# Two VectorE transposes moved behind a projection's additions in a paged-attention kernel

## The chip, the cores and the metric

The kernel runs on one core of a Trainium2 chip. The time is device microseconds (us) of one execution of the whole program; the median of three runs is taken. A separate execution is profiled, and times within it are counted from the start of its span.

## The reference

Two layers are added to x (8 sequences of 128 tokens, width 512, float32). The first is a projection by an adapter chosen for each sequence, followed by a small mixture of low-rank experts. The second, which takes nearly all of the time, is attention over a paged cache, followed by a gated low-rank network. The attention, cut to what matters:

```
q = x Wq  (32 heads of 128)    k = x Wk,  v = x Wv  (8 heads of 128)
q, k = rope(rmsnorm(q)), rope(rmsnorm(k))
k_all = concat(k_cache[block_table], k)        # 512 cached + 128 new keys
scores = q k_all / sqrt(128), cached keys beyond cache_seqlens masked
o = softmax(scores) v_all                      # v_all likewise
attention = o Wo                               # 32*128 -> 512
```

Four query heads share one key and value head.

## The kernel before

The attention is cut into 64 units (NU = 64): a unit is one sequence and one key head with its four query heads. `iteration(u)` (from line 1418 on) issues everything of unit u, and pieces of its neighbours, in an order written out by hand. Nothing reorders it later: each engine takes its instructions in the order of the program, and each waits at its own semaphores. TensorE is PE below, VectorE is DVE, ScalarE is ACT, GpSimd is POOL and SyncE is SP.

A unit has a loop `for h in range(REP)` over its four heads ("slots" 0 to 3). In a slot,

- `scores(u, h)` (lines 439 and 442) has PE multiply one head's queries with 512 cached and 128 new keys, into one of two PSUM tiles that take turns;
- `mask_exp(u, h)` (line 452) has DVE scale, mask and find the lowest value, and ACT take the exponential and its sum (line 463);
- `normalize(u, h - 1)` has DVE take the reciprocal of the previous head's sum (line 468) and POOL multiply by it (line 469);
- `blocks(u, h - 2)` (line 474) has DVE transpose a finished head's probabilities in blocks of 32, into the tile pb;
- `output(u - 3, h)` (line 1148) has PE multiply an older unit's result with a quarter of Wo;
- `project(k, j, slots[h - 1 : h])` has PE compute one of seven products of later units' q, k and v (line 262, two matmuls with half of the contraction each, recorded as four), and DVE add it from PSUM into the sums that it belongs to (line 265). Seven products stand for eight, as in Strassen's scheme. In slots 1, 2 and 3 these are the products 1, 2 and 6 in the odd units, and 4, 5 and 3 in the even ones; product 7 comes at the end of the odd units. Product 2 needs one addition, product 5 needs two.

In slot 2, `new_pb(u)` takes the tile pb. There is one such tile, so its first writer waits until the previous unit's transfer out of it is done. `blocks_qk(u + 2, u)` (line 425) is that first writer: DVE transposes the rotated queries and the key of unit u + 2 in blocks into it. `blocks(u, 0)` follows.

After the loop come the last reciprocal, the last two heads' blocks, `exchange_out(u)` and the rotation of unit u + 3 (lines 329 to 347). `exchange_out` writes pb to a tile px in DRAM, half from SP's and half from ACT's queue (line 486). In the next iteration `exchange_in` reads it back by SP's queue, reordered: qkb (line 1000), from which ACT makes the transposed queries of unit u + 2 (line 1010), and pT (line 1003), the transposed probabilities, which PE multiplies with the values two units later (line 1023). SP also loads the cached keys of the next sequence's units, kt, page by page (line 193): five or so ahead of `exchange_in` and three behind it in the odd units. POOL gathers the values (line 203), computes the sums of the weights' quarters (line 163) and of x, and issues the loads of weights.

Of the kernel before, what the change touches and what calls it, by code (L numbers as in the profile page):

```python
# [58 lines left out]
def adaln_ffn_kernel(  # L59
# [115 lines left out]
    def load_o(hf, *parts):  # L175

        for i, to in parts:
            nc.gpsimd.dma_start(out=wo_t[:, to], in_=wo[hf, i])
# [35 lines left out]
    def bank(tag, name):  # L214
        return ps_1.tile([P, DM], F32, tag=tag, name=name)
# [11 lines left out]
    NU = len(units)  # L227
# [25 lines left out]
    def project(k, j, products):  # L253

        pr, g = k % (B // 2), k // (B // 2) * GH + j
        key = k, j
        for i in products:
            x, y, tag = PRODUCTS[i]
            ps = bank(tag, f"p_{k}_{j}_{i}")[:, :HW]
            w = wq_t[g][:, y].rearrange("p (c n) -> p c n", c=2)  # L260
            for c in range(2):
                nc.tensor.matmul(  # L262
                    out=ps, lhsT=xo[:, pr, x, c, :], rhs=w[:, c, :], start=(c == 0), stop=(c == 1)
                )
            add = lambda out, a: nc.vector.tensor_tensor(out, a, ps, ALU.add)  # L265
            if i == 1:
                part_t[key] = pj.tile([P, HW], F32, tag="u", name=f"u_{k}_{j}")
                nc.scalar.copy(part_t[key], ps)
                c_t[4 * k + j] = pj.tile([P, 2 * HW], F32, tag="c0", name=f"c0_{k}_{j}", bufs=2)
                c_t[4 * k + 2 + j] = pj.tile([P, 2 * HW], F32, tag="c1", name=f"c1_{k}_{j}", bufs=2)  # L270
            u, c0, c1 = part_t[key], c_t[4 * k + j], c_t[4 * k + 2 + j]
            if i == 2:
                add(c0[:, :HW], u)
            elif i == 6:
                add(u, u)
            elif i == 7:
                add(c1[:, HW:], u)
            elif i == 4:
                add(c1[:, :HW], c1[:, HW:])
            elif i == 5:  # L280
                add(c1[:, HW:], c1[:, HW:])
                add(c0[:, HW:], u)
            elif i == 3:
                add(c0[:, HW:], c0[:, HW:])
# [71 lines left out]
    def transpose_qk(u, home=None):  # L356

        qk = qk_t.pop(u)
        t = banks(f"tq_{u}", 1 if u < 2 else None)
        for h in range(NH):  # L360
            nc.tensor.transpose(
                t[:, h * S : (h + 1) * S], qk[:, h].rearrange("p t d -> p (t d)"), ident
            )
        if home is None:
            home = pj.tile([P, NH * S], F32, tag="qkT", name=f"qkT_{u}", bufs=2)
        nc.scalar.copy(home, t[:, : NH * S])
        qkT_t[u] = home.rearrange("p (h s) -> p h s", h=NH)
# [55 lines left out]
    def blocks_qk(u, w):  # L423

        nc.vector.transpose(  # L425
            pb_t[w][:, :, PW:].rearrange("p i (h a) -> p h i a", a=32),
            qk_t.pop(u).rearrange("p h t d -> p h (t d)").rearrange(
                "p h (i a) -> p h i a", a=32
            ),
        )  # L430
# [3 lines left out]
    def scores(u, h, which=None):  # L434
        st, g = units[u]
        kt, _ = kv_t[st]
        qkT = qkT_t[u]
        s = banks(f"s_{u}_{h}", which)
        nc.tensor.matmul(  # L439
            out=s[:, :L], lhsT=qkT[:, h, :], rhs=kt[:, :, g % GH, :], start=True, stop=True  # L440
        )
        nc.tensor.matmul(  # L442
            out=s[:, L:NK], lhsT=qkT[:, h, :], rhs=qkT[:, REP, :], start=True, stop=True
        )
        s_t[u, h] = s

    def mask_exp(u, h):

        st, g = units[u]
        p = pp.tile([P, NK], F32, tag="p", name=f"p_{u}_{h}")  # L450
        low = stat.tile([P, 1], F32, tag="low", name=f"low_{u}_{h}")
        nc.vector.tensor_tensor_reduce(  # L452
            out=p,
            in0=s_t.pop((u, h))[:, :NK],
            in1=mask_t[st],
            scale=rs_t[u][:, h : h + 1],
            scalar=BIG,
            op0=ALU.add,
            op1=ALU.min,
            accum_out=low,  # L460
        )
        den = stat.tile([P, 1], F32, tag="den", name=f"den_{u}_{h}")
        nc.scalar.activation(p, p, AF.Exp, bias=low, scale=-1.0, accum_out=den)  # L463
        p_t[u, h], den_t[u, h] = p, den

    def normalize(u, h):
        den = den_t.pop((u, h))
        nc.vector.reciprocal(den, den)  # L468
        nc.gpsimd.tensor_scalar(p_t[u, h], p_t[u, h], den, 1.0, ALU.mult, ALU.mult)  # L469

    def blocks(u, h):

        w = (LC + 1) * 32
        nc.vector.transpose(  # L474
            pb_t[u][:, :, h * w : (h + 1) * w].rearrange("p i (j a) -> p j i a", a=32),
            p_t.pop((u, h)).rearrange("p (j i a) -> p j i a", i=QD, a=32),
        )
# [370 lines left out]
    def f_fold():  # L848

        nc.vector.tensor_copy(fw_t["s"], fw_t["f"])  # L850
# [141 lines left out]
    with ExitStack() as l1:  # L992
# [352 lines left out]
        def f_turn_of(b):  # L1345
            yT_t[b] = f_turn(b, *room(b))
# [71 lines left out]
        def iteration(u):  # L1418
            nonlocal room2

            on = lambda v: 0 <= v < NU
# [65 lines left out]
            for h in range(REP):  # L1487
                if on(u):
                    if (u, h) not in ((1, 0), (1, 1), (2, 0)):
                        scores(u, h)  # L1490
                        mask_exp(u, h)
                    if h > 0 and (u, h) != (1, 1):
                        normalize(u, h - 1)

                    if (u, h) == (1, 2):
                        transpose_qk(3)

                    sums_o(u, h)
                    sums_w(u, h)
                    if 16 <= u < NU - 8 and (r, h) == (2, 3):  # L1500
                        load_o(u // 16, (1, B12))

                    if h == 2:
                        new_pb(u)
                        if u + 2 in range(4, NU):
                            blocks_qk(u + 2, u)
                    if h > 1:
                        blocks(u, h - 2)
                    if h == 1 and u == NU - 5:
                        f_fold()  # L1510
                    if u == NU - 5 and h == 1:
                        t4 = wo_t[:, 6, : 2 * (E1 + HN)].rearrange("p (c n) -> p c n", c=2)
                        fw_t["qa"], qa_steps[:] = quarters_of(
                            fw_t["a"],
                            *quarter_rooms(wo_t[:, 5]),
                            t4[:, :, E1:],
                            t1_room.rearrange("p (c n) -> p c n", c=2),
                        )
                        sa = fw_t["sa"]
                        fw_t["qa"][M1], fw_t["qa"][M2] = (sa[:, c : c + 2, : E1 + HN] for c in (0, 2))  # L1520
                        fw_t["qa"][M4] = t4
                    at = (u - NU + 5, h)
                    if at == (1, 0):
                        nc.vector.tensor_copy(fw_t["qa"][M4][:, :, :E1], fw_t["s"][:, 2:])
                    if at in ((0, 1), (0, 2), (1, 0), (1, 1)):
                        qa_steps.pop(0)()
                    if u in GATED and h == 1:
                        f_add(GATED[u])
                    if u in GATED and h == 2:
                        f_mult(GATED[u])  # L1530
                    if h == 3:
                        z_blocks(u)
                    if h == 2 and u in FIRST:
                        f_turn_of(2 * FIRST[u])
                    if u in REST:
                        if h == 1:
                            f_turn_of(2 * REST[u] + 1)
                        elif h > 1:
                            f_step(REST[u], 2 * h - 4, 2 * h - 3)
                elif u in GATED and u < NU + 2:  # L1540
                    if h == 1:
                        f_add(GATED[u])
                    elif h == 2:
                        f_mult(GATED[u])
                    elif h == 3:
                        z_blocks(u)
                if on(u - 3):
                    output(u - 3, h)
                    sums_a(u - 3, h)
                if u in REST and h == 3:  # L1550
                    f_rest_products(REST[u], 0)
                if h > 0 and slots:
                    project(k, j, slots[h - 1 : h])

                if (u, h) in WHOLE:
                    project_whole(1, *WHOLE[u, h])
# [220 lines left out]
```

## Time and profile before

| what | value |
| --- | --- |
| runs | 1198.29, 1198.89 and 1201.55 us; median 1198.89 |
| the profiled execution | 1203.57 us, of which its span is 1201.8 us |
| granted clock of PE | 1.0 throughout |
| PE busy from 174 to 1054 us | 874.36 of 880 us |
| DVE busy in the same stretch | 720.22 us |
| POOL busy in the same stretch | 613.75 us |
| DMA share in the same stretch | 0.85 |
| DVE transposes of line 425, from 174 to 1054 us | 54, median 826 ns |
| DVE transposes of line 474, from 174 to 1054 us | 216, median 826 ns |
| DVE additions of line 265, from 174 to 1054 us | 189 of 128x384, medians 518 to 553 ns |

The stretch from 174 to 1054 us is given because units 5 to 58 lie in it; unit 4 has its first scores at 160.0 us. In rows of the order of time, the first column is the start and the second the duration; a bracket at the end holds the engine's idle time ahead of the row and what ended it. In lists of waits the three numbers are the sum, the number of times and the longest, the first and the last in us. The ends of matmuls are modelled, and their starts are not.

### The profile page before, as it was taken

The page shows a single profiled execution, that of the slowest core. Times are in us where ns is not written, and L with a number is a line of the kernel's source. Part 1 is how long each engine was busy: PE and PEld are TensorE (multiplying, and loading weights), DVE is VectorE, ACT ScalarE, POOL GpSimd, SP SyncE. Part 2 cuts the span into 40 slices and gives each one's busy share as a digit, 9 for nine tenths or more (in the row PEclk, how much of TensorE's full clock was granted, in tenths as well). Part 3 has the DMA queues.
Part 4 walks back from the last instruction along what each step waited for, and adds up shares of the span by engine and source line. Part 5 has one row for each costly group of instructions (what it writes and reads, how often), then busy time and mean ns, then how long its engine had stood idle before and what let it go on. Part 6 is the DMA issues. An engine that isn't in the chain of part 4 may idle for free.

```text
span 1201.8 us, 17007 instructions
## 1 busy us (share of the span) xinstructions
PE 1188.7 (99%) x4196; PEld 721.8 (60%) x4196; DVE 936.6 (78%) x2141; ACT 509.3 (42%) x1469; POOL 771.6 (64%) x867
## 2 busy tenths in 40 slices
PE   9999999999999999999999999999999999999998
PEld 7766555565655556555555555565655555655567
DVE  2557788787978887878888787878888888897757
ACT  1345544444444444434444344444444444444321
POOL 3554879778746676678656685677656684765432
PEclk9999999999999999999999999999999999999999
DMA  8823787888779978898889978888789878888643
GB/s 316 312 72 119 249 248 241 265 281 281 235 248 262 322 239 272 269 287 273 248 254 286 276 241 282 284 272 267 245 256 303 274 249 252 270 289 262 197 153 114
DMA packets 205447, 302.35 MB, mean 252 GB/s; under 512 B 84771, under 2 KB 119332, under 8 KB 204324
## 3 DMA queue, kind: packets, MB, share of 16 engines
q1 hardware_dynamic: 170164, 196.29, 53.2%
q10 hardware_dynamic: 18864, 52.57, 13.4%
q0 software_dynamic: 16320, 52.40, 12.5%
q8 instruction: 34, 0.56, 0.2%
q14 instruction: 65, 0.53, 0.1%
HBM read 185.44 MB, written 115.74 MB: 251 GB/s over the span
## 4 chain that ended last, share of the span: by engine, by line
PE 82%; DMA 5%; DVE 4%; POOL 4%; issue 2%; SPq 2%; ACT 1%; ACTq 0%; DVEq 0%; POOLq 0%
PE o L1023 18%; PE p L262 17%; PE s L439 15%; PE y L1148 12%; PE s L442 4%; DMA kt<-in_kc 3%; PE p L295 3%; PE cp L627 2%; PE bp L649 2%; PE y L1161 2%; DMA px<-pb 2%; DVE pb L474 1%; POOL p L469 1%; SPq L192 1%; PE op L981 1%
## 5 line engine op out<-in xcount | busy, mean ns | idle before, releaser
L463 ACT ACTIVATE p<-p,low 128x640 f32<-128x640 f32 x256 | 211.9, 828 | 428.5 <-DVE den L468 268.9
L469 POOL TENSOR_SCALAR p<-p,den 128x640 f32<-128x640 f32 x256 | 210.2, 821 | 219.5 <-DVE den L468 218.3
L452 DVE CUSTOM_DVE_ANT_0 p<-s,mask,rs 128x640 f32<-128x640 f32 x256 | 222.8, 879 | 82.8 <-PE s L442 82.0
L262 PE MATMUL p<-wqkv,xo 128*128 128x384 f32 x784 | 281.0, 487 | 1.3 <-POOL wqkv L163 0.7
L439 PE MATMUL s<-kt,qkT 128*128 128x512 f32 x504 | 258.3, 594 | 4.7 <-DMA px<-pb 1.7
L1023 PE MATMUL o<-pT,vt 128*128 128x512 f32 x512 | 230.3, 592 | 0.0
L474 DVE STREAM_TRANSPOSE pb<-p 128x640 f32<-128x640 f32 x248 | 204.8, 826 | 24.8 <-POOL p L469 24.7
L1148 PE MATMUL y<-wo,oT 128*128 128x256 f32 x784 | 206.5, 380 | 1.2 <-DVE yp L1217 1.0
L262 PEld LDWEIGHTS p<-wqkv,xo 128*128 128x128 f32 x784 | 148.3, 190 | 70.7 <-POOL wqkv L163 1.9
L442 PEld LDWEIGHTS s<-qkT 128*128 128x128 f32 x504 | 95.8, 190 | 120.5 <-issue 120.5
L203 POOL DMA_INDIRECT vt<-in_vc,vrow x128 | 138.3, 1081 | 42.0 <-issue 30.1
L1023 PEld LDWEIGHTS o<-pT,vt 128*128 128x128 f32 x512 | 97.0, 190 | 108.0 <-issue 92.8
L439 PEld LDWEIGHTS s<-kt,qkT 128*128 128x128 f32 x504 | 94.5, 190 | 77.1 <-issue 33.9
L1148 PEld LDWEIGHTS y<-wo,oT 128*128 128x128 f32 x784 | 131.9, 191 | 10.1 <-PE s L442 1.5
L311 ACT ACTIVATE sq<-c 128x128 f32<-128x128 f32 x320 | 98.8, 309 | 9.5 <-DVE oT L474 1.4
L442 PE MATMUL s<-qkT 128*128 128x128 f32 x504 | 96.8, 274 | 0.0
L317 POOL TENSOR_TENSOR rs<-ss,mhalf 128x5 f32<-128x5 f32 x64 | 84.0, 1312 | 5.3
L1046 ACT COPY oT<-o 128x512 f32<-128x512 f32 x64 | 37.5, 585 | 111.0 <-PE o L1023 92.4
L315 POOL TENSOR_SCALAR ss<-ss,eps 128x5 f32<-128x5 f32 x64 | 23.4, 366 | 73.1 <-ACT sq L311 73.1
L265 DVE TENSOR_TENSOR c<-c,p 128x384 f32<-128x384 f32 x84 | 44.9, 534 | 26.7 <-PE p L262 26.7
L1023 PE MATMUL o<-pT,vn 128*128 128x512 f32 x128 | 65.4, 592 | 0.0
L425 DVE STREAM_TRANSPOSE pb<-ca 128x640 f32<-128x640 f32 x60 | 49.9, 832 | 14.5 <-DMA kt<-in_kc 8.9
(301 smaller groups left out, 1513.8 us busy)
## 6 DMA issues: line engine op xcount, KB each, us to landing
pT<-px SPq DMA_DIRECT2D x64, 1280.0 KB, 7.3
px<-pb SPq DMA_DIRECT2D x120, 400.0 KB, 5.5
px<-pb ACTq DMA_DIRECT2D x120, 400.0 KB, 5.5
qkb<-px SPq DMA_DIRECT2D x60, 320.0 KB, 3.6
kt<-in_kc SPq DMA_DIRECT2D x512, 32.0 KB, 4.8
wqkv<-in_wqkv POOLq DMA_DIRECT2D x32, 384.0 KB, 5.1
wo<-in_wo POOLq DMA_DIRECT2D x17, 512.0 KB, 7.7
yd<-yp POOLq DMA_DIRECT2D x12, 512.0 KB, 9.1
```

Of the source, the lines that this page charges most:

```text
L203: nc.gpsimd.indirect_dma_start(out=kv_t[step][1][:, c, :], out_offset=None, in_=vc, in_offset=bass.IndirectOffsetOnAxis(ap=vrow[:, hf, at ...
L262: nc.tensor.matmul(out=ps, lhsT=xo[:, pr, x, c, :], rhs=w[:, c, :], start=(c == 0), stop=(c == 1))
L311: nc.scalar.activation(sq, cs[:, at : at + D], AF.Square, accum_out=ss[:, h : h + 1])
L317: nc.gpsimd.tensor_tensor(rs, ss, mhalf, ALU.pow)
L439: nc.tensor.matmul(out=s[:, :L], lhsT=qkT[:, h, :], rhs=kt[:, :, g % GH, :], start=True, stop=True)
L442: nc.tensor.matmul(out=s[:, L:NK], lhsT=qkT[:, h, :], rhs=qkT[:, REP, :], start=True, stop=True)
L452: nc.vector.tensor_tensor_reduce(out=p, in0=s_t.pop((u, h))[:, :NK], in1=mask_t[st], scale=rs_t[u][:, h : h + 1], scalar=BIG, op0=ALU.add, ...
L463: nc.scalar.activation(p, p, AF.Exp, bias=low, scale=-1.0, accum_out=den)
L469: nc.gpsimd.tensor_scalar(p_t[u, h], p_t[u, h], den, 1.0, ALU.mult, ALU.mult)
L474: nc.vector.transpose(pb_t[u][:, :, h * w : (h + 1) * w].rearrange("p i (j a) -> p j i a", a=32), p_t.pop((u, h)).rearrange("p (j i a) -> ...
L1023: nc.tensor.matmul(out=o, lhsT=vt[:, c, j * D : (j + 1) * D] if c < LC else vn_t.pop(u), rhs=pT[:, c], start=(c == 0), stop=(c == LC),)
L1148: nc.tensor.matmul(out=y_t["y"][:, half * HN : (half + 1) * HN], lhsT=part(key)[:, i * S : (i + 1) * S], rhs=wo_t[:, slot(w, key[0] // (B ...
```

## The change

In the units 4 to 58 (`3 < u < NU - 5`) the two transposes of slot 2, `blocks_qk(u + 2, u)` and `blocks(u, 0)`, are issued after that slot's `output` and `project` in place of before them. On DVE, which takes part in `project` with its additions, this places the one or two additions of slot 2 ahead of the two transposes; the order of the other engines' instructions stays. The other units keep the old order.

```
                     if h == 2:
                         new_pb(u)
-                        if u + 2 in range(4, NU):
+                    behind = h == 2 and 3 < u < NU - 5
+                    if h > 1 and not behind:
+                        if h == 2 and u + 2 in range(4, NU):
                             blocks_qk(u + 2, u)
-                    if h > 1:
                         blocks(u, h - 2)
...
                 if h > 0 and slots:
                     project(k, j, slots[h - 1 : h])
 
+                if on(u) and behind:
+                    blocks_qk(u + 2, u)
+                    blocks(u, 0)
+
                 if (u, h) in WHOLE:
                     project_whole(1, *WHOLE[u, h])
```

## What was predicted, with its working

> **What bounds the kernel now.** I read the page's busy table first, then the list of what TensorE (PE) waited for in the stretch from 174 to 1054 us, which holds nearly all of the units 4 to 58 that the change touches, and then the order of time around one unit.
>
> ```profile
> PE 1188.7 (99%) x4196; PEld 721.8 (60%) x4196; DVE 936.6 (78%) x2141; ACT 509.3 (42%) x1469; POOL 771.6 (64%) x867
> ```
>
> ```profile
> PE s L439 <- DMA px<-pb: 1.7, 1, 1.7
> PE s L439 <- DMA kt<-in_kc: 1.6, 2, 1.2
> PE y L1148 <- DVE yp L1217: 1.0, 1, 1.0
> PE p L262 <- POOL wqkv L163: 0.7, 1, 0.7
> PE s L439 <- DVE low L452: 0.2, 1, 0.2
> ```
>
> PE is busy 99% of the span, and over these 880 us all of its waits together are 1.7 + 1.6 + 1.0 + 0.7 + 0.2 = 5.2 us, in six places. Matmuls start back to back in between: four of line 262 at 619.92 and the next scores at 621.22, 1.30 us or 0.33 us a matmul, and this spacing recurs in every unit. The change moves no matmul. So it can win at most 5.2 us, and it can lose only where it makes PE wait.
>
> The Trainium skill speaks against reading the 99% so: "Perfetto Trace Analysis", section "Identifying the Most-Contended Engine", holds that matmul busy time is a poor measure of headroom and that the weight-load share is a better one. That share is 60% here, so by the rule the bound of a gain would not be 5.2 us but some 40% of the stretch, 352 of 880 us as an estimate from that page. The trace's unbroken start times say that none of it can be won by moving VectorE's work; I go by the trace, and the sum below does.
>
> **The profile's own time and the median.** The profiled execution took 1203.57 us, of which 1201.8 is its span and 1.8 lies around it. Without the 5.2 us it would be 1198.4. The median of the runs shown is 1198.89 and the lowest 1198.29. If the rest costs the same there, the median run holds only about 0.5 us of such waits: the late transfers of the profile are mostly not in it. I make each sum against 1203.57 first and then say what it leaves of 1198.89.
>
> **The order within one unit.** The change adds and removes no instruction. In 55 units it takes two VectorE transposes (line 425, the next query block, and line 474, the first head's block) from ahead of the h=2 projection's additions (line 265) to behind them. Unit 32, all engines in order of time:
>
> ```profile
> 619.69 0.89 DVE L452 CUSTOM_DVE_ANT_0 p<-s,mask,rs 128x640 f32<-128x640 f32 x1 [0.53 <-PE s L442]
> ...
> 619.92 1.45 PE L262 MATMUL p<-wqkv,xo 128*128 128x384 f32 x4
> ...
> 620.50 0.16 DVE L468 RECIPROCAL den<-den 128x1 f32<-128x1 f32 x1
> 620.58 0.83 DVE L425 STREAM_TRANSPOSE pb<-ca 128x640 f32<-128x640 f32 x1
> ...
> 621.33 0.80 DVE L474 STREAM_TRANSPOSE pb<-p 128x640 f32<-128x640 f32 x1
> ...
> 622.05 0.52 DVE L265 TENSOR_TENSOR c<-c,p 128x384 f32<-128x384 f32 x1
> ...
> 622.49 0.54 DVE L265 TENSOR_TENSOR c<-u,p 128x384 f32<-128x384 f32 x1
> ...
> 622.96 0.87 DVE L452 CUSTOM_DVE_ANT_0 p<-s,mask,rs 128x640 f32<-128x640 f32 x1
> ```
>
> The reader is to see that today the transposes fill the time in which PE computes the projection (619.92 to 621.37), and that the additions find it ready.
>
> **The added wait, step by step.** After the change the additions come first. VectorE is free at 620.66 and the projection ends at 621.37: a wait of 0.7 us. The two additions take 0.91 (622.05 to 622.96), the two transposes 1.47 (620.58 to 622.05), so the fourth head's mask (line 452) starts at about 621.4 + 0.91 + 1.47 = 623.8, 0.8 later than 622.96. In unit 31 the projection (603.99 + 1.45 = 605.44) ends 1.15 after the reciprocal (604.13 + 0.16 = 604.29); one addition follows, and the mask that started at 606.56 starts at 605.5 + 0.5 + 1.5 = 607.5, 0.9 later. From the same rows the delay of the fourth mask is about 0.8 where the unit's number divides by four, 1.2 where the remainder is two, 0.9 where it is three. Where it is one it is 1.2 less the time that line 425 already waits today.
>
> That last wait is what the change can win back. Line 425 writes the one buffer pb, and sits until the previous unit's transfer has left it. VectorE's list of waits in the same stretch has this under two names of one queue, 8.9 us in 8 cases and 3.9 in 5:
>
> ```profile
> DVE pb L425 <- DMA kt<-in_kc: 8.9, 8, 1.8
> ...
> DVE pb L425 <- DMA px<-pb: 3.9, 5, 1.1
> ```
>
> Behind the additions, these 13 waits run beside them. In unit 28 it is 1.8 us (until 556.17): both additions fit inside, and the fourth mask comes some 0.9 earlier.
>
> **Who is behind the waiting additions.** On VectorE: two transposes, the fourth mask, two reciprocals, the last transposes and the rotation. Through them ScalarE's fourth exponential and its squares, GpSimd's last two normalizations and its rs, and the exchange on SP's and ScalarE's queues: SP waited for line 474 at line 486 in 54 units, 182.0 us in all. So px goes out later by what is left at the unit's end: 0.8 (remainders 0 and 2, the latter after 0.4 us of today's wait before the h=3 additions), 0.45 (3), 0 to 1.2 (1).
>
> What PE sees of this is the next unit's first mask, which must free a PSUM bank before the third head's scores. In unit 33 the mask's accumulator is read by 632.08 and PE starts these scores at 633.49: 1.4 us of room, 0.8 used. From the same two rows in each unit, most others have 0.7 to 2.5 us. Three have under 0.5: 28 (none), where GpSimd's wait of 1.47 us ahead of the last transpose of unit 27 (546.47) sets the time and not VectorE; 45 (0.2), which follows a unit in which line 425 waits 1.1 us today and so gains; and 52 (0.5), where ScalarE waits 1.4 us for qkb. I count them at 0, and at up to 0.8 each if such a cover fails. VectorE's own waits in the next unit (in unit 32, 0.48 before the second mask and 0.76 before the additions) then take the delay away, so nothing piles up. The exception is unit 5, where PE waits 0.21 us already (178.13): it would wait 0.8 longer, **+0.8**. The bank of the h=2 projection is free earlier, which is worth nothing: no PE row waits for it in this stretch.
>
> **The key pages.** After px lands, SP issues qkb, pT and then the last three key pages, which the next even unit's first scores need:
>
> ```profile
> 672.82 7.08 DMA kt<-in_kc
> 679.90 0.51 issue
> 680.40 1.10 PE s L439 x2
> ```
>
> In this piece of the chain of waits the page takes 7.08 us and PE starts as soon as it is there. From the trace's landing times the last page comes less than 0.8 us ahead of the scores, or after they could start, in six units where px is also due later: 18, 26, 34, 36, 42 and 52. If 0.8 later at px were 0.8 later at the page, this costs 0.8 + 0.4 + 0.7 + 0.8 + 0.8 + 0.0 = **3.5** in the profiled execution. If the queue is full anyway (the DMA share is 0.85 here), or if the pages are as early as the median's missing waits suggest (by 0.4 to 1.7 us at units 18, 36 and 42), it costs **0**. I take 0 for the median, since its time leaves no room for the waits that make these places tight.
>
> The 1.0 us before line 1148 (unit 29, whose y bank VectorE frees late in unit 28) may go: between **0 and -0.9**, 0 if GpSimd's 0.53 us wait at 562.04 sets it. The 0.7 for line 163 is GpSimd's own work: 0.
>
> **Sum and rivals.** Profile's own time: 1203.57 + 0.8 + (0 to 3.5) - (0 to 0.9). From the median: 1198.89 + 0.8 = **1199.7**, no change that can be told.
>
> - *Absorbed* (the forecast): delay of 0.8 a unit, swallowed by the next; 1198.9 to 1200.5, centre 1199.7. For it: 5.2 us of PE waits in 880 us, although VectorE waits 68.6 us for scores. Chance 0.50.
> - *Slower, by the key pages*: px leaves 0.8 us later and the last pages land as much later. It decides wherever a page lands less than 0.8 us ahead of the scores. Price 0.8 + 3.5 = 4.3: 1203.2 from the median. For it: SP waits for VectorE in 54 of 55 units. Against: the median's time has no room for waits at these places. Failing covers at units 28, 45 and 52 belong here too. Chance 0.22.
> - *The waits for pb are won*: unit 28's late y and the px waits go and unit 5 costs little; the time is that without PE waits, 1198.3. Chance 0.25. This is also how it looks if the change does nothing, because the additions' new wait and the transposes' old one cancel.
> - *All PE waits go, and the median held them*: 1198.89 - 5.2 = 1193.7. The lowest run, 1198.29, speaks against it. Chance 0.03.
>
> **How the numbers follow.** A measurement of this kernel can tell about 0.3%, 3.6 us, from no change: 1195.3 to 1202.5 is "the same". Forecast and third case lie inside, 0.75; the key pages mostly outside, 0.22 slower; 0.03 faster. The range runs from 1198.0, just under the time without PE waits, to 1203.3, the key-page case; what is left out is the fourth case and the part of the second in which the delay adds up beyond its price.
>
> **What the profile after would show.** Line 265 of VectorE waits for PE in nearly all of 55 units, 0.7 or 1.15 us each, 40 us more than today's 32.3; line 425 waits for transfers hardly at all; the fourth mask's wait for scores is gone; SP's wait at line 486 grows. PE's waits stay near 5 us, with unit 5's at about 1. The prediction is wrong if PE shows new waits for line 452 beyond unit 5 or for kt in more than three units, or if its matmuls' start spacing changes.

## The result and the profile after

The changed kernel takes 1212.75 us (median of six runs, 1211.26 to 1214.14) beside 1201.05 us for the kernel before (1198.29 to 1202.46). The ratio is 1.0099, 95% interval 1.0086 to 1.0112: slower by 11.7 us between the medians. 1199.7 was predicted, in a range that ended at 1203.3. The profiled execution of the changed kernel took 1212.48 us with a span of 1210.7.

The page's busy table and PE's list of waits from 175 to 1063 us, which are about the same units as before:

```profile
PE 1190.9 (98%) x4196; PEld 720.9 (60%) x4196; DVE 941.8 (78%) x2141; ACT 504.8 (42%) x1469; POOL 775.0 (64%) x867
```

```profile
PE s L439 <- DMA kt<-in_kc: 3.6, 3, 1.3
PE y L1148 <- DVE yp L1217: 2.2, 4, 0.9
PE p L262 <- POOL wqkv L163: 1.7, 2, 1.2
PE s L439 <- DVE low L452: 1.3, 1, 1.3
PE y L1148 <- DVE yp L1235: 0.9, 1, 0.9
PE s L439 <- ACT oT L1046: 0.8, 1, 0.8
PE s L439 <- PE o L1023: 0.6, 2, 0.3
```

The work is the same, and PE's waits rise from 5.2 to 11.1 us. They come from four places that have nothing in common in the program: key pages, the y bank, GpSimd's sums of weights, and unit 5's first mask (the 1.3 of line 452). The last two rows are first scores as well (units 32, 36 and 50): the list names what came last by the profile, and the last packets of the key pages end 0.95 to 1.12 us ahead of these scores, as they do ahead of those that the list gives to kt (0.97 to 1.17 us in units 18, 34 and 52).

VectorE's waits in the same stretch, where the change was meant to act, before (174 to 1054 us) and after:

```profile
DVE p L452 <- PE s L442: 68.6, 86, 2.3
DVE c L265 <- PE p L262: 26.0, 37, 1.2
...
DVE u L265 <- PE p L262: 6.3, 16, 0.4
```

```profile
DVE c L265 <- PE p L262: 69.3, 72, 1.3
DVE p L452 <- PE s L442: 29.7, 49, 1.0
...
DVE pb L425 <- DMA kt<-in_kc: 1.4, 3, 0.6
```

The additions wait 37.0 us more than the 32.3 of before. The query block's wait for pb fell from 12.8 to 1.4, and the masks' wait for scores from 68.6 to 29.7: VectorE now comes to more of the masks later than PE. Unit 32 again, VectorE in order of time:

```profile
625.32 0.88 DVE L452 CUSTOM_DVE_ANT_0 p<-s,mask,rs 128x640 f32<-128x640 f32 x1 [0.53 <-PE s L442]
...
627.04 0.55 DVE L265 TENSOR_TENSOR c<-c,p 128x384 f32<-128x384 f32 x1 [0.75 <-PE p L262]
627.52 0.55 DVE L265 TENSOR_TENSOR c<-u,p 128x384 f32<-128x384 f32 x1
627.98 0.84 DVE L425 STREAM_TRANSPOSE pb<-ca 128x640 f32<-128x640 f32 x1
628.74 0.80 DVE L474 STREAM_TRANSPOSE pb<-p 128x640 f32<-128x640 f32 x1
629.68 0.88 DVE L452 CUSTOM_DVE_ANT_0 p<-s,mask,rs 128x640 f32<-128x640 f32 x1
```

From the third head's mask to the fourth's it is now 629.68 - 625.32 = 4.36 us; it was 622.96 - 619.69 = 3.27. The fourth mask is 1.09 us later, of which 0.75 is the new wait.

PE's list of waits counts only idle time after the modelled end of a matmul. A sharper account goes by starts: each matmul's distance to the one before it, less the spacing that recurs (429 ns behind 512 columns, 323 behind 384, 217 behind 256, 112 behind 128), where that is over 90 ns. For units 4 to 58, in us:

| what PE was late for | before | after |
| --- | --- | --- |
| first scores of unit 4, due before the change acts | 0.81 | 1.74 |
| first scores of the other units (key pages) | 4.28 | 6.13 |
| third scores of unit 5 (first mask) | 0.48 | 1.59 |
| other scores | 0.10 | 0.42 |
| output products, line 1148 (y bank) | 1.51 | 4.14 |
| projections, line 262 (mostly line 163's sums) | 1.53 | 2.74 |
| sum | 8.70 | 16.76 |

The 8.1 us between these sums are nearly all of the 8.9 between the two spans. 0.9 of them are unit 4's first scores, which the change can't have made late.

How late VectorE is can be counted from each unit's first scores. By the median over units 5 to 58 the third mask starts at the same time as before (0.0), the fourth 1.16 us later, and the unit's last transpose ends 0.99 us later.

**How VectorE's delay reaches the y bank.** Three engines at the end of unit 40 of the changed kernel, GpSimd, VectorE and PE:

```profile
761.85 0.80 POOL L469 TENSOR_SCALAR p<-p,den 128x640 f32<-128x640 f32 x1 [3.56 <-DVE den L468]
762.60 1.58 POOL L153 DMA_DIRECT2D wqkv<-in_wqkv  x2
764.18 0.84 POOL L469 TENSOR_SCALAR p<-p,den 128x640 f32<-128x640 f32 x1
```

```profile
765.06 0.84 DVE L474 STREAM_TRANSPOSE pb<-p 128x640 f32<-128x640 f32 x1 [1.31 <-POOL p L469]
765.83 1.18 DVE L1217 TENSOR_TENSOR yp<-yp,y 128x1024 f32<-128x1024 f32 x1
```

```profile
767.15 1.10 PE L1148 MATMUL y<-wo,oT 128*128 128x256 f32 x4 [0.87 <-DVE yp L1217]
```

GpSimd waits for VectorE's third reciprocal, multiplies, issues two weight loads (1.58 us), and only then multiplies for the fourth head; VectorE's last transpose waits for that, the addition that frees the y bank comes after it, and PE waits 0.87. Before, the same addition ran from 758.98 to 760.16 and PE needed the bank at 760.39:

```profile
758.98 1.18 DVE L1217 TENSOR_TENSOR yp<-yp,y 128x1024 f32<-128x1024 f32 x1
```

There was 0.2 us of room. Counted from the unit's first scores (745.10 and 750.83), the third head's multiplication starts 9.91 us in before, and 11.02 after: 1.1 later, and the wait follows at units 9, 25 and 41.

### The profile page after: what moved, and what is told of

Its sections match the earlier page's. It is cut to its first block, busy times and chain, and to the rows that moved or that the text cites. A ratio compares the mean times of both kernels' runs of the same rounds, so it can differ in the third digit from the quotient of the medians.

```text
span 1210.7 us, 16952 instructions
## 1 busy us (share of the span) xinstructions
PE 1190.9 (98%) x4196; PEld 720.9 (60%) x4196; DVE 941.8 (78%) x2141; ACT 504.8 (42%) x1469; POOL 775.0 (64%) x867
## 4 chain that ended last, share of the span: by engine, by line
PE 79%; DVE 6%; DMA 5%; POOL 4%; issue 3%; SPq 2%; ACT 1%; ACTq 0%; DVEq 0%; POOLq 0%
PE p L262 17%; PE o L1023 16%; PE s L439 15%; PE y L1148 12%; PE s L442 4%; DMA kt<-in_kc 3%; PE p L295 3%; PE cp L627 2%; PE bp L649 2%; PE y L1161 2%; POOL p L469 1%; DVE pb L474 1%; SPq L192 1%; DMA px<-pb 1%; DVE p L452 1%
## 5 line engine op out<-in xcount | busy, mean ns | idle before, releaser
L203 POOL DMA_INDIRECT vt<-in_vc,vrow x128 | 138.5, 1082 | 36.1 <-issue 32.3
L1148 PEld LDWEIGHTS y<-wo,oT 128*128 128x128 f32 x784 | 131.8, 191 | 12.8 <-PE s L442 4.1
L265 DVE TENSOR_TENSOR c<-u,p 128x384 f32<-128x384 f32 x84 | 46.0, 548 | 30.2 <-PE p L262 30.2
```

What stands on the lines that cost most here:

```text
L203: nc.gpsimd.indirect_dma_start(out=kv_t[step][1][:, c, :], out_offset=None, in_=vc, in_offset=bass.IndirectOffsetOnAxis(ap=vrow[:, hf, at ...
L1148: nc.tensor.matmul(out=y_t["y"][:, half * HN : (half + 1) * HN], lhsT=part(key)[:, i * S : (i + 1) * S], rhs=wo_t[:, slot(w, key[0] // (B ...
```

## The experiments

The theory after the result: the additions' wait makes VectorE about 1 us late in each unit; that lateness costs nothing on VectorE itself and leaves through whatever is due behind it. Rivals: the wait or the new order costs in itself; a late pb, by the query block, costs; one exit carries it all. Kernels of one group shared a chip and its runs of the kernel before, and each ratio is against those. The expected times were written against a kernel before of about 1201 us; the groups' medians for it were 1200.4 to 1202.1.

| kernel | median us | ratio | 95% interval |
| --- | --- | --- | --- |
| the change | 1212.75 | 1.0099 | 1.0086 to 1.0112 |
| projection first | 1207.97 | 1.0054 | 1.0036 to 1.0073 |
| query block alone behind | 1205.23 | 1.0029 | 1.0013 to 1.0044 |
| first head's block alone behind | 1207.31 | 1.0048 | 1.0033 to 1.0063 |
| delay alone, old order | 1217.41 | 1.0129 | 1.0108 to 1.0149 |
| change, late addition earlier | 1215.48 | 1.0121 | 1.0096 to 1.0146 |
| change, key pages ahead to unit 57 | 1208.24 | 1.0062 | 1.0041 to 1.0083 |
| before, key pages ahead to unit 57 | 1203.89 | 1.0022 | 1.0006 to 1.0039 |
| change, both of these edits | 1208.21 | 1.0064 | 1.0043 to 1.0086 |
| change in odd units alone | 1204.27 | 1.0022 | 1.0006 to 1.0039 |
| change in even units alone | 1216.82 | 1.0126 | 1.0099 to 1.0154 |
| before, key pages ahead in all | 1201.61 | 1.0001 | 0.9984 to 1.0017 |
| that, query block behind in a quarter | 1204.82 | 1.0025 | 1.0007 to 1.0043 |
| change, key pages ahead in all | 1209.18 | 1.0063 | 1.0041 to 1.0085 |
| that, not in weight units | 1204.60 | 1.0022 | 1.0003 to 1.0040 |
| that, in weight units alone | 1206.83 | 1.0045 | 1.0029 to 1.0060 |

**Is it the wait, the order, or the lateness?** Three kernels vary the wait, one makes VectorE late without it.

Projection first, on the changed kernel:

```
+                first_p = on(u) and behind
+                if first_p and slots:
+                    project(k, j, slots[h - 1 : h])
                 if on(u - 3):
                     output(u - 3, h)
                     sums_a(u - 3, h)
...
-                if h > 0 and slots:
+                if h > 0 and slots and not first_p:
                     project(k, j, slots[h - 1 : h])
```

> The changed kernel, but in units 4 to 58 PE computes slot 2's projection ahead of that slot's output product, so the additions' wait is shorter by the output's 0.43 to 0.87 us; the two transposes stay behind the additions. Theory (the additions' wait makes VectorE late, and that lateness is what costs): the wait falls from 0.7 or 1.15 to about 0.3 us, so most of the 11.8 us go, 1201 to 1205. Rival (the new place of the transposes costs, whatever the wait: a later pb and exchange): 1210 to 1213.

Query block alone behind (for the head's block alone, the two calls change places):

```
-                    if h > 1 and not behind:
-                        if h == 2 and u + 2 in range(4, NU):
-                            blocks_qk(u + 2, u)
+                    if h == 2 and u + 2 in range(4, NU) and not behind:
+                        blocks_qk(u + 2, u)
+                    if h > 1:
                         blocks(u, h - 2)
...
                 if on(u) and behind:
                     blocks_qk(u + 2, u)
-                    blocks(u, 0)
```

> Only the query block (line 425) is moved behind the additions; the first head's block stays ahead. Theory (lateness by the wait): the head's block of 0.75 us fills the wait, which leaves 0 to 0.4 us a unit, and waits for pb of some 12 us in all are shortened: 1199 to 1203. Rival (it is the query block's lateness, through pb, that costs): near the changed kernel, 1210 to 1213.

> Only the first head's block (line 474) is moved behind the additions; the query block stays ahead. Theory (lateness by the wait): the query block fills the wait and 0 to 0.4 us a unit are left: 1200 to 1204, a little above the kernel with the query block behind, since the waits for pb stay. Rival (it is the head's block that must not be late): near the changed kernel, 1210 to 1213.

Delay alone, on the kernel before:

```
+                            if 3 < u < NU - 5:
+                                again = u + 2, qk_t[u + 2]
                             blocks_qk(u + 2, u)
...
                     project(k, j, slots[h - 1 : h])
+                if h == 2 and 3 < u < NU - 5:
+                    qk_t[again[0]] = again[1]
+                    blocks_qk(u + 2, u)
```

> The kernel before with its order, and the query block done a second time behind slot 2's additions in units 4 to 58: VectorE is 0.75 us later there with no new wait for PE. Theory (lateness alone costs, whatever makes it): most of the loss is there without the change, 1206 to 1213. Rival (the wait for PE, or the new order, costs): 1200 to 1203, as before.

The delay alone costs 1.29%, as much as the change or more and above the range that I had expected, with the old order and the additions' wait lower than before (11.9 us at line 265). So lateness is enough; neither the wait nor the order is needed. The second block is also written into pb, so px is late there too, and line 425's waits for pb rise from 12.8 to 32.0 us: this kernel doesn't tell by which path the lateness costs. With the projection first the additions' wait falls from 69.3 to 35.7 us and the loss to 0.54%: half, where I had expected most of it to go. Either transpose left in front fills the wait in part; each kernel loses less than the change, though more than I had expected, and neither block stands out as the one that must not be late.

The lateness itself, the end of a unit's last transpose counted from its first scores as above, is 0.99 us with the change, 0.93 with the delay alone, 0.33 with the first head's block behind, 0.20 with the projection first and 0.02 with the query block behind. The two late kernels lose the most, 0.99 and 1.29%. The three others still lose 0.29 to 0.54%, and what they lose it by is open.

The query block behind does not win the waits for pb back either. Line 425 hardly waits any more (0.2 us), but the first head's block, left in front, is now the first to write pb and has the wait:

```profile
DVE pb L474 <- DMA kt<-in_kc: 9.7, 9, 1.8
...
DVE pb L474 <- DMA px<-pb: 2.2, 4, 0.7
```

Before, line 474 had no row of this kind in its list from 174 to 1054 us, and line 425 had 12.8 us.

**Which exits?** Two edits close one exit each, on the changed kernel and one also on the kernel before.

Late addition earlier, in the units 8, 12, 24, 28, 40 and 44 (and, by the same condition, 56):

```
                 blocks(u, REP - 2)
+                early = 3 < u < NU - 5 and r in (8, 12)
+                if early:
+                    add_output(u - 3, True)
                 blocks(u, REP - 1)
                 exchange_out(u)
-            if on(u - 3):
+            if on(u - 3) and not (on(u) and early):
                 add_output(u - 3, True)
```

> The changed kernel, with the late output addition (lines 1217 and 1235) ahead of the unit's last transpose in the units 8, 12, 24, 28, 40 and 44, where that transpose waits 0.5 to 1.3 us for GpSimd and the addition after it frees the y bank too late. Theory (part of the loss is the late y bank): PE's waits at line 1148, 3.1 us in the changed kernel's profile, go; the time falls by about 3 us, to 1209 or 1210. Rival (what PE waits for there is only moved to the next wait, because VectorE stays as late): 1212 to 1213.

Key pages ahead of pT (`exchange_in` calls `between` after the load of qkb and before that of pT):

```
-                exchange_in(u - 1)
-            if pages:
+                ahead_of = pages and u % GH == 1 and 3 < u < NU - 5
+                exchange_in(u - 1, (lambda: gather(st + 1, first + 5, end)) if ahead_of else None)
+            if pages and not (on(u - 1) and ahead_of):
                 gather(st + 1, first + 5, end)
```

> The changed kernel, with the last three key pages of the odd units 5 to 57 issued between qkb and pT and not behind pT. Theory (part of the loss is key pages that land late behind px, qkb and pT): PE's waits for kt, 3.6 us in the changed kernel's profile between 162 and 1070 us, go, and more where the run had more: 1207 to 1209.5. Rival (the pages are late because all transfers are, not because of their place): 1211 to 1213.

> The kernel before, with the last three key pages of the odd units 5 to 57 issued between qkb and pT. Theory: the waits for kt and px, 3.3 us in the profile of before, go: 1198 to 1200, near the time without PE waits. Rival (pT, moved back by three pages, is then late for something, or the pages were not what cost): 1201 to 1203.

> The changed kernel with both edits, the late output addition moved ahead and the key pages ahead of pT. Theory (the loss is the sum of two separate chains, with about a third for others such as line 163's sums and unit 5): 1205 to 1207. Rival (one chain stands behind both, VectorE's lateness, which finds another wait): above 1209.

With the pages ahead no first scores of the units 5 to 58 are late any more, by starts 0 in place of 6.1 us, and the loss falls from 0.99 to 0.62%, or 4.4 us: a part of it leaves by the key pages. Moving the late addition gains nothing, with the pages ahead or without, where I had expected some 3 us. PE's waits from 175 to 1063 us, with the key pages ahead, without that edit and with it (behind line 1003 the lines of these kernels have numbers higher by two):

```profile
PE s L439 <- DVE low L452: 2.7, 4, 1.3
PE y L1150 <- DVE yp L1219: 1.7, 2, 0.9
PE p L262 <- POOL wqkv L163: 1.6, 2, 1.2
PE y L1150 <- DVE yp L1237: 0.9, 1, 0.9
```

```profile
PE p L262 <- POOL wqkv L163: 4.1, 5, 1.2
PE s L439 <- DVE low L452: 1.6, 2, 1.3
```

The waits for y go (2.6 us, by starts 3.8) and waits for GpSimd's sums of weights come (1.6 to 4.1, by starts 2.6 to 5.6). The new ones stand in units 13, 29 and 45, the units behind 12, 28 and 44, which are among those that the edit touches. GpSimd in unit 13, without the edit and with it:

```profile
305.64 0.27 POOL L315 TENSOR_SCALAR ss<-ss,eps 128x5 f32<-128x5 f32 x1 [1.22 <-ACT sq L311]
306.00 1.20 POOL L317 TENSOR_TENSOR rs<-ss,mhalf 128x5 f32<-128x5 f32 x1
```

```profile
305.47 0.79 POOL L315 TENSOR_SCALAR ss<-ss,eps 128x5 f32<-128x5 f32 x1 [1.22 <-ACT sq L311]
306.33 1.52 POOL L317 TENSOR_TENSOR rs<-ss,mhalf 128x5 f32<-128x5 f32 x1
...
314.69 1.81 POOL L163 TENSOR_TENSOR wqkv<-wqkv 128x768 f32<-128x768 f32 x1
```

```profile
316.56 2.85 PE L262 MATMUL p<-wqkv,xo 128*128 128x384 f32 x8 [0.82 <-POOL wqkv L163]
```

Both chains begin 0.41 us after the unit's first scores (305.23 and 305.06), when ScalarE's squares are done. With the edit the first two instructions take 0.84 us more; GpSimd then has no gap of over 0.3 us, and the sum that PE waits for ends 11.45 us after the first scores in place of 10.69. What changed beside these two is VectorE's work: without the edit it does the late output step (line 1237, from 305.22 to 306.41) at that time, and with it the rotation's line 329 (from 305.54 to 306.79). In all kept traces together, line 317 takes over 1.35 us in 312 of the 328 cases in which it begins while line 329 runs, or up to 0.1 us before, and in none of the 760 others. So the edit closes one exit and makes GpSimd late by itself in three units, for about as much as it wins. Whether the y bank and the weight sums are separate prices that add up, as my theory had it, this pair of kernels doesn't decide.

**Which units?** The change in the odd or in the even units alone adds `and u % 2 == 1` or `and u % 2 == 0` to the definition of `behind`.

> The change in the odd units 5 to 57 alone. Theory (lateness costs only where something is due right behind it: the last key pages behind an even unit's px, the y bank after units 8, 24 and 40, the first mask of unit 5): the odd units cost little, 1200 to 1203. Rival (every unit's lateness costs about the same): half of the loss, 1206.

> The change in the even units 4 to 58 alone. Theory: nearly the whole loss, 1209 to 1213. Rival (every unit's lateness costs about the same): half of it, 1206.

The even units cost 1.26%, more than expected, the odd ones 0.22%, and the whole change no more than the even ones alone. The rival of equal parts fails. This fits the exits: the last key pages wait behind an even unit's px, the y bank of units 9, 25 and 41 behind units 8, 24 and 40, and unit 5's first mask behind unit 4. It is not a clean test of them, since the two kernels aren't equally late. With the change in the even units alone, odd units that leave 1 when divided by 4 end their last transpose 0.99 us later as well, by the median and though nothing is changed in them: line 425 waits for pb 19.3 us in all there, in odd units alone, and 12.8 before. With the change in the odd units alone, these end 0.6 us later and the even units 0.0.

**Can the pages be a gain by themselves?** The run of the kernel before with the pages ahead up to unit 57 was slower by 0.22%, where I had expected a small gain; it had PE wait 2.4 us for kt at units 60 and 62, whose last pages were still issued behind pT. So `3 < u < NU - 5` became `u > 3`:

> The kernel before, with the last three key pages ahead of pT in all odd units from 5 on, the units 59 and 61 too, where the run that stopped at 57 had PE wait 2.4 us for kt. Theory (those 2.4 us were the whole reason why that run gained nothing): 1198 to 1201. Rival (pT is late for something else): 1203 to 1204, as there.

and with that, the query block alone behind where `u % 4 == 1`:

> The kernel before with the key pages ahead of pT in all odd units from 5 on, and the query block alone behind the additions in the units whose number leaves 1 when divided by 4, where line 425 waits 0.5 to 1.3 us for pb. Theory (the change is right where the wait for pb is longer than the wait that it brings): at or below the kernel with the pages alone, 1197 to 1200. Rival (VectorE is late there too): above it, 1202 to 1205.

The first is level with the kernel before (1.0001). Its first scores are late nowhere in units 5 to 58, 4.3 us won by starts, and its y products and projections are late by 7.6 us in place of 3.0. So PE may only meet the next waits where the pages no longer hold it up; but in the run with the pages ahead up to unit 57 the same two came to 4.2 us, and how much of the 7.6 is that one execution's is open. The second kernel is slower by 0.25%. It doesn't test what I meant it to, for the wait for pb moves here too: where the query block is behind, line 474 waits for px and kt in its place (1.6 and 5.3 us). No version here beats the kernel before.

**What is left with the pages ahead.** The change with the pages ahead in all odd units, then without the change in unit 4 and the units whose number leaves 7 to 13 when divided by 16 ("weight units"), then in those alone. I had miscounted them: the rule takes in 55 to 58 too, where no weights are loaded, so it is 26 units and 29 others, not 21 and 34.

```
-                    behind = h == 2 and 3 < u < NU - 5
+                    behind = h == 2 and 3 < u < NU - 5 and not (u == 4 or 7 <= r <= 13)
```

> The changed kernel with the last three key pages ahead of pT in all odd units from 5 on. Both theories: as with the pages moved up to unit 57, 1206 to 1209; it is the measure for the next two.

> The same, with the change left out in unit 4 and in the units whose number leaves 7 to 13 when divided by 16, in which GpSimd also loads and sums weights: 34 of 55 units keep it. Theory (what is left of the loss goes through GpSimd's chain in those units and through unit 5's first mask): as the kernel before with these pages, 1200 to 1203. Rival (it is spread over all units): 1204 to 1206.

> The same, with the change in unit 4 and in those 21 units alone. Theory: the whole rest of the loss, 1206 to 1209. Rival (spread over all units): 1203 to 1204.

They add up: 0.22% and 0.45% beside 0.63%. About two thirds come from the 26 units, which is more than their share, and one third from the others, though the two intervals overlap; neither theory holds alone. Which waits make up that third is open: the profiled executions behind 1209.18 and 1201.61 differ by only 2.5 us, less than the medians, and show no single place for it.

## Why the prediction was wrong, point by point

- **The added wait: right in kind, a little small.** Foreseen were 40 us more at line 265, measured 37.0; the fourth mask of unit 32 was to be 0.8 us later and is 1.09, and the end of a unit was to be 0 to 1.2 us later and is 0.99 by the median. The waits for pb went as foreseen (12.8 to 1.4 us).
- **"VectorE's own waits then take the delay away, so nothing piles up": right for VectorE, wrong as an answer.** By the third mask of the next unit the delay is gone (0.0 by the median), but each unit sends it on to SP, ScalarE and GpSimd before VectorE has made it good.
- **"I take 0 for the median": the step that failed first.** It rested on a floor of 1198.4 from PE's list of waits, and so on a median without late pages. By starts PE lost 8.7 us in units 4 to 58, not 5.2, which puts the floor of the profiled execution at 1194.9; the kernel before ran at 1195.97 in one later run, and its medians in the four later groups were 1200.4 to 1202.1. So the median had room for late pages, though no trace of a median run was kept to show them, and a delay of about 1 us met them: moving the pages takes 4.4 us of the loss away. I had priced that at 3.5, and given it to the rival with a chance of 0.22. That the price came so near is in part luck: of the six units that I listed, 18, 34 and 52 were later in the changed kernel's profile, 36 was earlier and 26 and 42 not late at all, while 20, 32 and 50 were new.
- **The y bank: an exit that was not in the sum.** I had only looked for a gain there, 0 to -0.9. By starts it was +2.6. Unit 40's rows show how it was missed: 0.2 us of room at 760.39, and GpSimd's wait of 1.3 us ahead of the last transpose, which I took in unit 27 as a cover that VectorE cannot move. GpSimd's work there begins with VectorE's reciprocal, so it moves as well.
- **GpSimd's sums of weights: "GpSimd's own work: 0".** By starts the projections lost 1.2 us more. In unit 43 GpSimd's line 315 begins 1.54 us later than before, counted from the first scores, and takes 1.23 us in place of 0.27, beside VectorE's line 329; PE waits 1.2 us for the sum there. So these sums hang on VectorE twice, by its lateness and by what it does beside them.
- **Unit 5: +0.8 foreseen, +1.1 measured** (0.48 to 1.59 by starts).
- **What the sum comes to.** Of the 0.99%, roughly 0.36 go with the pages, 0.41 by leaving out unit 4 and the weight units, and 0.22 stay with the other 29 units. The first is tied to one wait by an experiment; the y bank, the sums and unit 5 are seen in the starts of one profile, and no run closes one of them without moving something else.
- **The rule on matmul busy time** pointed at the right weakness: PE is 98 to 99% busy in both kernels, and that, with the list of waits, hid 3.5 us in the kernel before. The 352 us worked out from the rule appear in no run here.

The slower rival named the right first price but only one exit, and put the end of the range at 1203.3. The sum should have begun so: about 1 us late in 55 units, and each transfer, bank and sum that is due less than 1 us behind them pays.

## What to carry to other kernels

An engine with a fifth of its time idle may still be late where it matters: ask of a delay not whether the engine makes it good by the next round, but what it sends out before, and list the room of each receiver. A wait on another engine is a cover only if the other engine's work doesn't itself begin with the delayed one. Where one wait is removed and the time stays, look first whether the edit itself made something else late, as GpSimd's two short instructions here, before calling the new wait the next one of the same chain. An edit that moves the first writer of a buffer hands the wait to the next writer, as with pb. And judge a floor by the starts of the bottleneck's instructions, not by the idle time of a list.

## What the runs showed of the hardware

In either order the transposes took 0.83 to 0.84 us and the additions 0.52 to 0.55 by their medians, and PE's granted clock was 1.0. Two things I had not expected. GpSimd's short instruction of line 317 (five columns) takes some 1.20 us, and mostly 1.5 to 1.75 when it begins beside VectorE's line 329; line 315 takes 0.27 and then up to 1.35. And single runs spread far, which I put down to late transfers without a trace that shows it: the kernel with the query block behind ran between 1201.05 and 1210.41 us, and the kernel before between 1195.97 and 1206.90 over all groups. A profile is one such run; the profiles of two kernels can differ by less than their medians, as with 2.5 us beside 7.6 here.
